# Layer 0 of a four-layer graph network: weighted sum by rows, the gate's sum on VectorE, a fourth buffer for the adjacency

## The chip, the cores and the metric

The kernel runs on one core of a Trainium2 chip, as one program. The metric is the device time of one execution in microseconds, the median of several runs. A core has a matrix engine (TensorE, PE in the profile, with its weight loads shown apart as PEld), a vector engine (VectorE, DVE), an activation engine (ScalarE, ACT), a general engine (GpSimd, POOL) and an engine that mostly issues transfers (SyncE, SP). Each runs its own instructions in order; they wait for one another by semaphores. SBUF is the on-chip memory, PSUM the memory into which PE writes its products. Transfers are issued here from SP and from POOL.

## The reference, cut to what matters

There are 16 graphs (batches) of 1024 nodes with 128 features each, and a 1024x1024 adjacency of zeros and ones per graph, symmetric and with a full diagonal. Four layers follow one another, each with a residual and a layer norm. The change touches the first one, which computes per batch:

```python
h = x @ W_w.T + W_b
e = jnp.einsum('bjl,bkl->bjk', h @ A, h)
e = e + jnp.swapaxes(e, 1, 2)
att = jnp.where(adj > 0, e, -9e15)
att = softmax(att, axis=1) * adj
h_prime = relu(einsum('bij,bjk->bik', att, h))
coeff = sigmoid(concatenate([x, h_prime], axis=-1) @ gate_w.T + gate_b)
x = layernorm(x + coeff * x + (1 - coeff) * h_prime)
```

The scores are symmetric before the softmax, so a row of them can be normalised where a column is meant. The gate is one number per node: 256 products, 128 with x and 128 with h', and a sum. Layer 1 first removes neighbours from the adjacency in an iterative way (the dilation), and then runs three aggregations with batch norms; layers 2 and 3 are another attention and a graph convolution. Nothing in them is changed except the number of buffers of one small pool in the dilation.

## The kernel before, in words

A batch has NT = 8 tiles of P = 128 nodes. Layer 0 is written as three Python generators per batch, which are run in turns ("rounds"): each `yield n` hands the turn to the other streams and comes back n rounds later. In round order the streams are `before(b + 1)`, `attention(b)` and `after(b - 1)`, so that the preparation of one batch, the attention of the next and the end of the one before go on at once. The order in which instructions are emitted, with a planner's reordering within each engine, fixes the order on each engine.

`before(b)` loads x (`xn`, L925, issued on SP) and eight pieces of the adjacency (`an`, 128x1024, L930, also on SP). ACT turns each piece into 8-bit numbers in the large buffer `Y` (printed as `carry`) and sums it to the degree (L931). DVE compares each piece with its mirror image, for a check of symmetry, in rows of several lengths: one against SBUF (L936) and one or two against PSUM (L944), into which PE has written transposed blocks (L943). On the way PE transposes x (L759), ACT copies it to `xT` (L950), PE and ACT make `G` (L766, L954), PE makes the x half of the gate in `gates` (L775, then L780), and PE and DVE make `hn`, the rows of h (L962, L963). At the end POOL stores the 8-bit adjacency (L965).

`attention(b)` takes the eight tiles one after another (`jt`): ACT makes a mask (L980), PE the scores of 128 rows against 1024 columns in two halves (L724), DVE adds the mask and takes the row minimum (`em`, L983), ACT the exponential with its row sum (L985), DVE the reciprocal `rs` (L987) and `hs`, 128 rows of h divided by that sum (L989). `weigh`, called one tile late, multiplies `hs` with `em` and adds up in `acc` in PSUM over the eight tiles (L973): `hs` is the stationary operand, two halves of 512 columns of `em` are streamed, and the result stands with features on the partitions and nodes along the row.

`after(b)` closes a batch. The relu (L1001, ACT) writes `hpT`, features on partitions. Three rounds later `gates` multiplies it with the h' half of the gate's vector in four column tiles of PE (L775), ACT copies the result out (L777), PE transposes it (L780) and DVE adds the x half, `gx` (L1005). ACT's tanh (L1007) and two small DVE rows (L1009, L1010) give the factors `cx` and `co` per node. Three rounds later DVE multiplies x by `cx` (L1013), PE transposes `hpT` back in eight blocks (L759), DVE multiplies these by `co` (L1015) and adds (L1016). Four rounds later, in round 10 of the 17 that `attention` takes, comes the layer norm (`normed`: statistics L794 and L796 on DVE, a power on POOL L745, L799 on DVE, eight rows L801 on ACT), and POOL stores the result (L1019). The next x load on SP reuses that buffer and so waits for that store.

PSUM holds two buffers of 1024 columns for the scores (`l0_pw`), one for `acc`, and two of 512 columns (`l0_ph`), which the transposes, G, h and the gates share. `an` has three buffers, `xn` three, `em` two. After layer 0 the score pools are closed and the dilation begins (`prepare` and what follows from L1063); the end of the last batch, `after(15)`, runs among its first instructions. There POOL computes a power over all degrees (L1188), which is in POOL's queue ahead of the last layer norm's power.

Of the kernel before, what the change touches and what calls it, by code (L numbers as in the profile page):

```python
# [9 lines left out]
F32 = mybir.dt.float32  # L10
# [5 lines left out]
FP8 = mybir.dt.float8e4  # L16
# [6 lines left out]
P = 128  # L23
# [616 lines left out]
def fast_kernel(ctx: ExitStack, tc: tile.TileContext, t: dict, out: bass.AP, flag: bass.AP):  # L640
# [46 lines left out]
    def nat(ap):  # L687
        return ap.rearrange("(t p) d -> p t d", p=P)
# [39 lines left out]
    def tiles3(ap):  # L728
        return ap.rearrange("p (t d) -> p t d", d=P)
# [24 lines left out]
    def turned(psum, src, tag="h"):  # L754

        for p, c, blocks in halves(psum, tag):
            for i, k in enumerate(blocks):
                s = src[:, k, :] if len(src.shape) == 3 else src[:, k * P:(k + 1) * P]
                nc.tensor.transpose(p[:, i * P:(i + 1) * P], s, identf)  # L759
            yield p, c, slice(blocks[0], blocks[-1] + 1)  # L760
# [8 lines left out]
    def gates(psum, out, *pairs):  # L769


        p = psum.tile([P, N // 4], F32, name="pq", tag="h")
        for i, (g, x) in enumerate(pairs):
            for q in range(4):
                nc.tensor.matmul(p[32 * q:32 * q + 32, :], g, x[:, q * N // 4:(q + 1) * N // 4], start=(i == 0),  # L775
                                 stop=(i == len(pairs) - 1), tile_position=(0, 32 * q))
        nc.scalar.copy(out, p)  # L777
        p = psum.tile([P, 2, P], F32, name="pg", tag="h")
        for t in range(2):
            nc.tensor.transpose(p[:, t, :], out[:, t * P:(t + 1) * P], identf)  # L780
        return p.rearrange("p t (q g) -> p q t g", q=4)

    def half_rows(v):

        return v[:, :, None].to_broadcast([P, 4, P])
# [124 lines left out]
    work = ending.enter_context(tc.tile_pool(name="l0_work", bufs=1, reuse_waits="tile"))  # L910
    small = ending.enter_context(tc.tile_pool(name="l0_small", bufs=2, reuse_waits="tile"))
    b0 = row_bcast(wts, t["L0_gnn_W_b"], P, "l0brow")
    gw = wts.tile([P, 2, 32], F32, name="l0gw")
    nc.vector.memset(gw, 0.0)
    with nc.allow_non_contiguous_dma(reason="a vector of 256"):
        nc.sync.dma_start(gw[:, :, 0], t["L0_gnn_gate_w"].rearrange("o (h d) -> d (o h)", d=P))
    gb = row_bcast(wts, t["L0_gnn_gate_b"], 1, "l0gb")
    gbh = wts.tile([P, 1], F32, name="l0gbh")
    nbig = wts.tile([P, 1], F32, name="l0nbig")
# [2 lines left out]
    def before(s, b):  # L922

        s.xn = work.tile([P, NT, P], F32, name="xn", bufs=3)
        nc.sync.dma_start(s.xn, nat(t["x"][b]))  # L925
        yield 1
        for it in range(NT):
            c = b * NT + it
            an = early.tile([P, N], F32, name="an", bufs=3)
            nc.sync.dma_start(an, t["adj"][b][it * P:(it + 1) * P, :])  # L930
            nc.scalar.activation(Y[b][:, it, :], an, AF.Copy, accum_out=deg[:, c:c + 1], saturate=False)  # L931

            chk = early.tile([P, N], FP8, name="chk")
            done = (it + 1) * P
            if done < N:
                nc.vector.scalar_tensor_tensor(chk[:, done:], an[:, done:], 0.0, an[:, done:], op0=OP.is_gt,  # L936
                                               op1=OP.not_equal, accum_out=other[:, b, it:it + 1], saturate=False)
            for h in range(it // 4 + 1):
                js = range(4 * h, min(4 * h + 4, it + 1))
                k = slice(js[0] * P, (js[-1] + 1) * P)  # L940
                pt = ps_h.tile([P, 512], F32, name="pt", tag="h")
                for i, jt in enumerate(js):
                    nc.tensor.matmul(pt[:, i * P:(i + 1) * P], Y[b][:, jt, it * P:done], identb, start=True, stop=True)  # L943
                nc.vector.scalar_tensor_tensor(chk[:, k], pt[:, :k.stop - k.start], 0.0, an[:, k], op0=OP.is_gt,  # L944
                                               op1=OP.not_equal, accum_out=other[:, b, 7 + it + 4 * h:8 + it + 4 * h],
                                               saturate=False)
            if it == (2 if b else 0):
                s.xT = work.tile([P, N], F32, name="xT", bufs=2)
                for p, c, _ in turned(ps_h, s.xn):
                    nc.scalar.copy(s.xT[:, c], p)  # L950
            if it == (4 if b else 1):
                s.G = work.tile([P, N], F32, name="G", bufs=2)
                for p, c in products(ps_h, (M0, s.xT)):
                    nc.scalar.activation(s.G[:, c], p, AF.Identity, scale=-1.0, bias=nu)  # L954
                pz = gates(ps_h, early.tile([P, N], FP8, name="chk").bitcast(F32), (gw[:, 0, :], s.xT))
                s.gx = small.tile([P, NT], F32, name="gx")
                nc.vector.tensor_copy(s.gx.rearrange("p (q t) -> p q t", t=2), pz[:, :, :, 0])
            if it == (5 if b else 2):
                s.hn = work.tile([P, N], F32, name="hn")
                for p, c, blocks in halves(ps_h):  # L960
                    for i, k in enumerate(blocks):
                        nc.tensor.matmul(p[:, i * P:(i + 1) * P], s.xT[:, k * P:(k + 1) * P], W0T, start=True, stop=True)  # L962
                    nc.vector.tensor_add(tiles3(s.hn[:, c]), tiles3(p), b0[:, None, :].to_broadcast([P, 4, P]))  # L963
            yield 2
        nc.gpsimd.dma_start(adj8_d[b], Y[b].bitcast(F32))  # L965

    def attention(s, b):
        s.acc = ps_a.tile([P, N], F32, name="acc")

        def weigh(jt, hs, em):  # L970
            for h in range(H2):
                c = slice(h * 512, (h + 1) * 512)
                nc.tensor.matmul(s.acc[:, c], hs, em[:, c], start=(jt == 0), stop=(jt == NT - 1))  # L973

        for jt in range(NT):
            js = slice(jt * P, (jt + 1) * P)
            c = b * NT + jt
            mn = mx0[:, c:c + 1]
            msk = work.tile([P, N], BF16, name="msk", bufs=2)
            nc.scalar.activation(msk, Y[b][:, jt, :], AF.Identity, scale=-BIG, bias=nbig)  # L980
            e = wide_matmul(ps_w, s.G[:, js], s.xT)
            em = work.tile([P, N], F32, name="em", bufs=2)
            nc.vector.tensor_tensor_reduce(em, e, msk, 1.0, 3.0e38, op0=OP.add, op1=OP.min, accum_out=mn)  # L983
            sm = small.tile([P, 1], F32, name="sm")
            nc.scalar.activation(em, em, AF.Exp, scale=-1.0, bias=mn, accum_out=sm)  # L985
            rs = small.tile([P, 1], F32, name="rs")
            nc.vector.reciprocal(rs, sm)  # L987
            hs = small.tile([P, P], F32, name="hs")
            nc.vector.tensor_scalar(hs, s.hn[:, js], rs, None, op0=OP.mult)  # L989
            yield  # L990
            if jt:
                weigh(*late)
            late = jt, hs, em
            yield
        weigh(*late)
        yield

    def after(s, b):

        hpT = work.tile([P, N], F32, name="hpT")  # L1000
        nc.scalar.activation(hpT, s.acc, AF.Relu)  # L1001
        yield 3
        pz = gates(ps_h, work.tile([P, NT, P], F32, name="r").rearrange("p t d -> p (t d)")[:, :N // 4], (gw[:, 1, :], hpT))
        co = small.tile([P, NT], F32, name="co")
        nc.vector.tensor_add(co.rearrange("p (q t) -> p q t", t=2), pz[:, :, :, 0],  # L1005
                             s.gx.rearrange("p (q t) -> p q t", t=2))
        nc.scalar.activation(co, co, AF.Tanh, scale=0.5, bias=gbh)  # L1007
        cx = small.tile([P, NT], F32, name="cx")
        nc.vector.tensor_scalar(cx, co, 0.5, 1.5, op0=OP.mult, op1=OP.add)  # L1009
        nc.vector.tensor_scalar(co, co, -0.5, 0.5, op0=OP.mult, op1=OP.add)  # L1010
        yield 3
        r = work.tile([P, NT, P], F32, name="r")
        nc.vector.tensor_mul(s.xn, s.xn, per_row(cx))  # L1013
        for p, c, k in turned(ps_h, hpT):
            nc.vector.tensor_mul(r[:, k, :], tiles3(p), half_rows(co[:, k]))  # L1015
        nc.vector.tensor_add(s.xn, s.xn, r)  # L1016
        yield 4
        normed(small, s.xn)
        nc.gpsimd.dma_start(nat(x1_d[b]), s.xn)  # L1019
        yield  # L1020
# [13 lines left out]

    with ExitStack() as ph:
        sb = ph.enter_context(tc.tile_pool(name="dl_sb", bufs=2, side="right", reuse_waits="tile"))
        tiny = ph.enter_context(tc.tile_pool(name="dl_small", bufs=3, side="right", reuse_waits="tile"))
        ps_b = ph.enter_context(tc.tile_pool(name="dl_pb", bufs=1, space=PSUM, side="right", reuse_waits="tile"))
        ps_d = ph.enter_context(tc.tile_pool(name="dl_pd", bufs=1, space=PSUM, side="right", reuse_waits="tile"))
        ps_s = ph.enter_context(tc.tile_pool(name="dl_ps", bufs=2, space=PSUM, side="right", reuse_waits="tile"))  # L1040
# [826 lines left out]
```

## Time and profile before

| what | value |
|---|---|
| median of 3 runs | 2696.75 us (2693.25 to 2697.32) |
| the profiled execution | 2694.93 us, span 2693.2 us, PE clock 0.983 of full speed |
| relu of batch 0, of batch 15 | 57.9 us, 624.9 us |
| a steady turn, relu to relu | 37.5 us |
| busy in one such turn (405.86 to 443.38) | PE all of it, ACT 33.3, DVE 30.2, POOL 3.2 us |
| issue to landing, median | `an` 3.7, x load 4.4, 8-bit adjacency store 4.2 us |

The profile is one execution. Line numbers (L973) are those of the kernel before. A row of the timeline has the start, the length, the engine, the line, the operation, what goes out and what comes in, the shapes and the count; in brackets the idle time of the engine before it and the engine that ended it. A row of the waits has who waited for whom, with the sum in us, the count and the longest. A row for a stretch of time has the busy time and the number of instructions of PE, PEld, DVE, ACT and POOL, then the clock that PE was granted, the share of the DMA engines and their GB/s. Lengths of single instructions contain time that overlaps the next one; the distance from one start to the next is what an engine spends on it.

### The profile page before, as it was taken

The page shows a single profiled execution, that of the slowest core. Times are in us where ns is not written, and L with a number is a line of the kernel's source. Part 1 is how long each engine was busy: PE and PEld are TensorE (multiplying, and loading weights), DVE is VectorE, ACT ScalarE, POOL GpSimd, SP SyncE. Part 2 cuts the span into 40 slices and gives each one's busy share as a digit, 9 for nine tenths or more (in the row PEclk, how much of TensorE's full clock was granted, in tenths as well). Part 3 has the DMA queues.
Part 4 walks back from the last instruction along what each step waited for, and adds up shares of the span by engine and source line. Part 5 has one row for each costly group of instructions (what it writes and reads, how often), then busy time and mean ns, then how long its engine had stood idle before and what let it go on. Part 6 is the DMA issues. An engine that isn't in the chain of part 4 may idle for free.

```text
span 2693.2 us, 41450 instructions
## 1 busy us (share of the span) xinstructions
PE 2539.0 (94%) x14888; PEld 1677.9 (62%) x14888; DVE 2085.4 (77%) x5590; ACT 1977.5 (73%) x3188; POOL 317.7 (12%) x287
## 2 busy tenths in 40 slices
PE   8999999997888869999999998999999999999986
PEld 4444454444666648887788885566566666666655
DVE  6887778876898877777688875678778777887885
ACT  7888889885988866666655534777777777777773
POOL 0000000003000001111122132001100100001010
PEclk9999999998999989999999998999999999999998
DMA  6555555530000052233366673102122111111100
GB/s 191 157 180 172 164 172 168 168 121 21 2 3 2 2 212 87 95 118 128 132 230 238 228 263 132 40 32 79 67 85 77 63 63 63 63 63 63 47 24 25
DMA packets 120807, 285.34 MB, mean 106 GB/s; under 512 B 12304, under 2 KB 65424, under 8 KB 113424
## 3 DMA queue, kind: packets, MB, share of 16 engines
q1 hardware_dynamic: 101280, 203.33, 23.1%
q0 software_dynamic: 19312, 79.28, 7.6%
q8 instruction: 119, 1.95, 0.3%
q14 instruction: 96, 0.79, 0.1%
HBM read 202.72 MB, written 79.82 MB: 105 GB/s over the span
## 4 chain that ended last, share of the span: by engine, by line
PE 58%; DVE 16%; issue 6%; ACT 4%; POOL 4%; DMA 2%; POOLq 0%; ACTq 0%; DVEq 0%
PE ph L1619 8%; PE acc L1679 7%; PE acc L1307 7%; PE ph L766 5%; PE acc L973 5%; PE pmm L724 5%; PE ph L759 4%; PE ph L1433 4%; PE pmm L1691 3%; PE ph L1606 2%; DVE mid L1097 2%; DVE keep L1148 2%; POOL ln_rstd L745 1%; POOL rn L745 1%; ACT q L1145 1%
## 5 line engine op out<-in xcount | busy, mean ns | idle before, releaser
L745 POOL TENSOR_TENSOR ln_rstd<-ln_rstd,mhalf 128x8 f32<-128x8 f32 (+1 forms) x68 | 108.3, 1593 | 1318.7 <-DVE ln_rstd L742 864.2
L973 PE MATMUL acc<-em,hs 128*128 128x512 f32 x512 | 259.3, 607 | 2.5 <-DVE past L1075 1.3
L724 PE MATMUL pmm<-xT,G 128*128 128x512 f32 x512 | 259.8, 604 | 0.0
L1679 PE MATMUL acc<-ex,hs 128*128 128x512 f32 x512 | 248.9, 596 | 7.5 <-DVE hs L1706 4.6
L801 ACT ACTIVATE xn<-xn,ln_nb,ln_rstd 128x128 f32<-128x128 f32 x512 | 204.6, 481 | 61.1 <-DVE ln_nb L799 61.0
L1307 PE MATMUL acc<-a,hi 128*128 128x512 f32 x768 | 232.7, 396 | 11.5 <-DVE a L1294 8.5
L1307 PE MATMUL acc<-a,lo 128*128 128x512 f32 x768 | 230.3, 394 | 5.9 <-DVE lo L1274 5.8
L985 ACT ACTIVATE em<-em,mx 128x1024 f32<-128x1024 f32 x128 | 146.3, 1143 | 54.0 <-DVE mx L983 52.7
L983 DVE CUSTOM_DVE_ANT_0 em<-pmm,msk 128x1024 f32<-128x1024 f32 x128 | 156.1, 1219 | 31.9 <-PE pmm L724 30.8
L1699 ACT ACTIVATE ex<-em,mn 128x1024 f32<-128x1024 f32 x128 | 146.9, 1148 | 44.7 <-DVE mn L1696 44.0
L1691 PE MATMUL pmm<-G,hT 128*128 128x512 f32 (+3 forms) x416 | 175.3, 523 | 0.1
L1696 DVE CUSTOM_DVE_ANT_0 em<-pmm,msk 128x1024 f32<-128x1024 f32 x128 | 155.4, 1214 | 24.4 <-PE pmm L1693 22.3
L1307 PEld LDWEIGHTS acc<-a,lo 128*128 128x128 f32 x768 | 143.1, 189 | 41.2 <-DVE lo L1274 12.0
L1307 PEld LDWEIGHTS acc<-a,hi 128*128 128x128 f32 x768 | 141.8, 189 | 42.9 <-DVE a L1294 11.0
L1157 ACT ACTIVATE carry<-pc,negone 128x1024 fp8e4<-128x1024 f32 x128 | 141.4, 1116 | 26.2 <-PE pc L1156 23.2
L931 ACT ACTIVATE carry<-an 128x1024 fp8e4<-128x1024 f32 x128 | 134.5, 1051 | 30.5 <-DMA an<-in_adj 29.7
L980 ACT ACTIVATE msk<-carry,l0nbig 128x1024 bf16<-128x1024 fp8e4 x128 | 145.4, 1136 | 0.0
L1619 PE MATMUL ph<-A,hi 128*128 128x512 f32 x512 | 143.1, 420 | 1.2 <-DVE zn L1608 0.7
L1687 ACT ACTIVATE msk<-A,nbig 128x1024 bf16<-128x1024 fp8e4 x128 | 144.2, 1137 | 0.0
L1296 ACT CAST a<-A 128x1024 fp32r<-128x1024 fp8e4 x96 | 98.4, 1048 | 54.3 <-PE acc L1307 52.7
L1679 PEld LDWEIGHTS acc<-ex,hs 128*128 128x128 f32 x512 | 88.6, 190 | 76.8 <-issue 54.6
L1296 ACT CAST a<-carry 128x1024 fp32r<-128x1024 fp8e4 x96 | 99.1, 1047 | 47.1 <-PE acc L1307 46.8
(319 smaller groups left out, 6185.2 us busy)
## 6 DMA issues: line engine op xcount, KB each, us to landing
an<-in_adj SPq DMA_DIRECT2D x128, 512.0 KB, 3.7
adj_d<-carry POOLq DMA_DIRECT2D x16, 1024.0 KB, 4.2
A<-dil_d SPq DMA_DIRECT2D x16, 1024.0 KB, 5.3
rdeg<-rdeg_d SPq DMA_DIRECT2D x32, 512.0 KB, 3.9
A<-adj_d SPq DMA_DIRECT2D x16, 1024.0 KB, 4.8
ag_d<-ag POOLq DMA_DIRECT2D x24, 512.0 KB, 5.0
ag<-ag_d SPq DMA_DIRECT2D x24, 512.0 KB, 5.3
xn<-in_x SPq DMA_DIRECT2D x16, 512.0 KB, 4.4
```

The lines of the kernel that those rows point to most:

```text
L724: nc.tensor.matmul(p[:, h * 512:(h + 1) * 512], lhsT, rhs[:, h * 512:(h + 1) * 512], start=True, stop=True)
L745: nc.gpsimd.tensor_tensor(r, r, mhalf[:, :n], op=OP.pow)
L801: nc.scalar.activation(r[:, k.start + i, :], r[:, k.start + i, :], AF.Identity, scale=rstd[:, i:i + 1], bias=nb[:, i:i + 1])
L973: nc.tensor.matmul(s.acc[:, c], hs, em[:, c], start=(jt == 0), stop=(jt == NT - 1))
L983: nc.vector.tensor_tensor_reduce(em, e, msk, 1.0, 3.0e38, op0=OP.add, op1=OP.min, accum_out=mn)
L1296: nc.scalar.copy(a, A[:, 2 * i:2 * i + 2, c])
L1307: nc.tensor.matmul(acc, part[:, jt, :], pieces[h * NT // 2 + k][:, jt - 2 * k, :], start=(part is parts[0] and jt == 0), stop=(part is par ...
L1619: nc.tensor.matmul(p, part[:, jt, :], A[jt][:, c], start=(jt == 0 and i == 0), stop=(jt == NT - 1 and i == 1))
L1679: nc.tensor.matmul(s.acc[:, c], hs, ex[:, c], start=(jt == 0), stop=(jt == NT - 1))
L1691: nc.tensor.matmul(e[:, c], s.hT[:, js], s.G[:, c], start=True, stop=True)
L1696: nc.vector.tensor_tensor_reduce(row, e, msk, 1.0, 0.0, op0=OP.add, op1=OP.min, accum_out=mn)
L1699: nc.scalar.activation(ex, row, AF.Exp, scale=-1.0, bias=mn, accum_out=sm)
```

## The change

`weigh` now takes a 128x128 block of `em` as the stationary operand and streams `hs`, so that there are eight products of 128 columns per tile instead of two of 512, and `acc` has nodes on the partitions and features along the row. The relu so writes `hp` by rows. The h' half of the gate is computed on DVE, for each of the eight blocks a multiplication with the gate's vector in all partitions (`ghrow`, a new small load) and a sum along the row (L1006 of the new kernel), two rounds behind the relu instead of three. There is no second `gates`, no copy of it and no transposes back; `hp` is multiplied by `co` in one instruction of 128x1024 (new L1014), in place, and added (new L1015). The layer norm comes in round 15 instead of 10. `an` has four buffers, the x load is issued on POOL for batches above 2, the gate's weights `gw` hold the x half only, and the dilation's small pool has two buffers instead of three.

```diff
-    gw = wts.tile([P, 2, 32], F32, name="l0gw")
+    gw = wts.tile([P, 32], F32, name="l0gw")
     nc.vector.memset(gw, 0.0)
-    with nc.allow_non_contiguous_dma(reason="a vector of 256"):
-        nc.sync.dma_start(gw[:, :, 0], t["L0_gnn_gate_w"].rearrange("o (h d) -> d (o h)", d=P))
+    nc.sync.dma_start(gw[:, 0:1], t["L0_gnn_gate_w"][:, :P].rearrange("o d -> d o"))
+    ghrow = row_bcast(wts, t["L0_gnn_gate_w"][:, P:], P, "l0gh")
...
-        nc.sync.dma_start(s.xn, nat(t["x"][b]))
+        (nc.gpsimd if b > 2 else nc.sync).dma_start(s.xn, nat(t["x"][b]))
...
-            an = early.tile([P, N], F32, name="an", bufs=3)
+            an = early.tile([P, N], F32, name="an", bufs=4)
...
-            for h in range(H2):
-                c = slice(h * 512, (h + 1) * 512)
-                nc.tensor.matmul(s.acc[:, c], hs, em[:, c], start=(jt == 0), stop=(jt == NT - 1))
+            for k in range(NT):
+                c = slice(k * P, (k + 1) * P)
+                nc.tensor.matmul(s.acc[:, c], em[:, c], hs, start=(jt == 0 and k % 4 == 0), stop=(jt == NT - 1 and k % 4 == 3))
...
-        hpT = work.tile([P, N], F32, name="hpT")
-        nc.scalar.activation(hpT, s.acc, AF.Relu)
-        yield 3
-        pz = gates(ps_h, work.tile([P, NT, P], F32, name="r").rearrange("p t d -> p (t d)")[:, :N // 4], (gw[:, 1, :], hpT))
+        hp = work.tile([P, NT, P], F32, name="hp")
+        nc.scalar.activation(hp, tiles3(s.acc), AF.Relu)
+        yield 2
+        r = work.tile([P, P], F32, name="r")
         co = small.tile([P, NT], F32, name="co")
-        nc.vector.tensor_add(co.rearrange("p (q t) -> p q t", t=2), pz[:, :, :, 0],
-                             s.gx.rearrange("p (q t) -> p q t", t=2))
+        for i in range(NT):
+            nc.vector.scalar_tensor_tensor(r, hp[:, i, :], 1.0, ghrow, op0=OP.mult, op1=OP.mult, accum_out=co[:, i:i + 1])
+        nc.vector.tensor_add(co, co, s.gx)
         nc.scalar.activation(co, co, AF.Tanh, scale=0.5, bias=gbh)
...
-        yield 3
-        r = work.tile([P, NT, P], F32, name="r")
+        yield 4
         nc.vector.tensor_mul(s.xn, s.xn, per_row(cx))
-        for p, c, k in turned(ps_h, hpT):
-            nc.vector.tensor_mul(r[:, k, :], tiles3(p), half_rows(co[:, k]))
-        nc.vector.tensor_add(s.xn, s.xn, r)
-        yield 4
+        nc.vector.tensor_mul(hp, hp, per_row(co))
+        nc.vector.tensor_add(s.xn, s.xn, hp)
+        yield 9
         normed(small, s.xn)
...
-        tiny = ph.enter_context(tc.tile_pool(name="dl_small", bufs=3, side="right", reuse_waits="tile"))
+        tiny = ph.enter_context(tc.tile_pool(name="dl_small", bufs=2, side="right", reuse_waits="tile"))
```

More of the change, by code (lines that the diff above doesn't have):

```diff
@@ L954, in before @@
                     nc.scalar.activation(s.G[:, c], p, AF.Identity, scale=-1.0, bias=nu)
-                pz = gates(ps_h, early.tile([P, N], FP8, name="chk").bitcast(F32), (gw[:, 0, :], s.xT))
+                pz = gates(ps_h, early.tile([P, N], FP8, name="chk").bitcast(F32), (gw, s.xT))
                 s.gx = small.tile([P, NT], F32, name="gx")
```

## The prediction

> **What bounds the kernel now.** I read the page's totals and its chain first, to see which engine sets the end.
>
> ```profile
> PE 2539.0 (94%) x14888; PEld 1677.9 (62%) x14888; DVE 2085.4 (77%) x5590; ACT 1977.5 (73%) x3188; POOL 317.7 (12%) x287
> ...
> PE 58%; DVE 16%; issue 6%; ACT 4%; POOL 4%; DMA 2%; POOLq 0%; ACTq 0%; DVEq 0%
> ...
> L973 PE MATMUL acc<-em,hs 128*128 128x512 f32 x512 | 259.3, 607 | 2.5 <-DVE past L1075 1.3
> ```
>
> TensorE carries the chain, and the line to be changed, L973, never waits inside layer 0. But these are averages, so I went to the stage. Layer 0 repeats one turn per batch; I measure it from one relu (L1001) to the next. These start at 57.9, 104.1, 142.2, 180.5, then every 37.5 us to 593.6, and last at 624.9. Next, one steady turn's busy times (PE, PEld, DVE, ACT, POOL), then its waits, then single instructions on PE, DVE, POOL and SP.
>
> ```profile
> 405.86:443.38 37.52, 37.52 (x158) 18.51 (x157) 30.23 (x98) 33.26 (x58) 3.17 (x3) 1.00 0.53 169
> ```
>
> ```profile
> DVE rs L987 <- ACT em L985: 4.9, 3, 2.0
> ...
> ACT carry L931 <- DMA an<-in_adj: 1.1, 2, 0.6
> ```
>
> ```profile
> 410.73 0.64 PE L775 MATMUL pq<-hpT,l0gw 128*32 128x256 f32 x8
> 411.30 1.12 PE L724 MATMUL pmm<-xT,G 128*128 128x512 f32 x2
> ...
> 416.16 0.60 PE L759 MATMUL ph<-identf,hpT 128*128 128x128 f32 x4
> 416.60 1.02 PE L724 MATMUL pmm<-xT,G 128*128 128x512 f32 x2
> ...
> 432.02 1.95 PE L962 MATMUL ph<-l0WT,xT 128*128 128x128 f32 x16
> 433.80 1.02 PE L973 MATMUL acc<-em,hs 128*128 128x512 f32 x2
> ```
>
> ```profile
> 409.81 0.29 DVE L944 SCALAR_TENSOR_TENSOR chk<-pt,an 128x128 fp8e4<-128x128 f32 x1
> 410.02 0.09 DVE L944 DVE_READ_ACCUMULATOR chk<-pt,an 128x1 bf16 x1
> 410.02 0.16 DVE L987 RECIPROCAL rs<-sm 128x1 f32<-128x1 f32 x1
> ```
>
> ```profile
> 433.20 0.91 POOL L1019 DMA_DIRECT2D x_d<-xn  x1 [3.88 <-ACT xn L801]
> ```
>
> ```profile
> 438.00 0.38 SPq L925 DMA_DIRECT2D xn<-in_x  x1
> ```
>
> ```profile
> 624.10 20.74 POOL L1188 TENSOR_TENSOR deg<-deg,mhalf 128x128 f32<-128x128 f32 x1 [5.87 <-DVE deg L1187]
> ...
> 646.49 0.17 DVE L799 SCALAR_TENSOR_TENSOR ln_nb<-ln_mv,ln_rstd 128x8 f32<-128x8 f32 x1 [5.80 <-POOL ln_rstd L745]
> ```
>
> The reader should see: PE is busy for the whole turn at full clock, DVE is free for 7 of its 37.5 us and ACT for 4, and an adjacency piece is late by at most 0.6 us without PE waiting. So PE instructions set the turn, until another engine is late. The starts in the PE rows give pitches: 416.16 to 416.60 is 0.11 us per transpose; 416.60 to 417.46 (the next row) is 0.43 per 512-column record; 432.02 to 433.80 is 0.111 for each of 16 records of L962. A block multiply of 128 columns on DVE shows 0.29 us but its successor starts 0.21 later.
>
> **What the Trainium skill says.** "FP8 and Floating Point Precision", TensorE Precision Notes: true FP32 takes four passes through the array. The trace agrees: a 512-column product is two records of 0.43, 0.86 us, which is four times 512 columns at 2.4 GHz (0.853). "TensorE: Matmul & The Clock Gate", Step-by-step: the next weights load while the current matmul runs. L962 agrees: a new 128x128 block of weights for each product and still 0.22 us per product. "VectorE: DVE Perf Modes", The TRN2 errata: (N+151)/0.96 ns for a two-operand fp32 operation, 291 ns at 128. The row's 0.29 agrees; start to start it is less, and I use the trace. "DMA: Bandwidth & Descriptors", Latency and other measured facts: first byte about 1 us from GpSimd against 0.6 us from Sync; the issues above (0.91 and 0.38) lean the same way.
>
> **The change, part by part**, per steady turn, durations from that turn.
> Removed on PE: the h' half of the gate, 8 records of L775, 0.57 with 0.2 for going into and out of column tiles, together 0.78; two L780 transposes, 0.22; eight L759 transposes of hpT, 0.87. Sum 1.87.
> Added on PE: L973 gives 64 products of 128 columns for 16 of 512. L962 has the same shape with changing weights, so 64 × 0.2225 = 14.24 against 32 × 0.429 = 13.73: +0.51. No trace shows this shape alternating with 512-column products. From below, equal streaming costs 0; from above, 0.24 per product gives +1.6. I take +0.51. Net on PE: -1.36, a turn of 36.16 if PE keeps streaming.
> ACT loses the copy of L777, 0.35. It has 4 us to spare; nothing gained.
> DVE loses two L1015 multiplies (0.64 each) and gains one of 1024 (1.15, as L1013) and eight block sums. One has the form of the check's 128-column row, 0.21 to 0.22 each. Bounds: no less than 0.15 (128 columns and the shortest neighbours), no more than 0.41 (0.29, an accumulator read of 0.085 and a hand-over, if nothing overlaps). I take 0.22: +1.76. DVE goes from 30.4 to 32.1 of 36.2.
>
> That fits as a sum, not everywhere: `yield 2` puts the sums early. In the new order all eight lie before the fifth minimum (L983) of the turn. Behind the first, which can start when the relu ends (relu + 1.04), come up to that minimum's end: 8 sums 1.76, 4 hs 0.88, 3 rs 0.37, check rows from PSUM 3 × 0.60 + 0.21 + 0.35 + 0.47 = 2.83, check rows from SBUF 1.02 + 0.88 + 0.74 + 0.60 + 0.47 = 3.71, 4 minima 4.66, the gate's small rows 0.35, the multiplies by cx and co 2.30. Sum 16.9, so it ends at relu + 17.9. It frees a score buffer that PE wants after 9 half-scores (7.72), 32 products of L973 (7.12), about 26 check transposes (1.45), 8 transposes of x (0.87) and switches (0.5): relu + 17.7. PE is 0.25 late. The check row behind it holds a PSUM slot for G (L953) and costs another 0.2. So the turn is 36.16 + 0.45 = 36.6, a saving of 0.9, and each 0.01 on a block sum costs 0.08.
>
> Transfers: the fourth adjacency buffer takes away at most the waits above, which PE doesn't feel, so 0 in a steady turn. The x load moves to POOL behind the x1 store. The norm now comes in round 15, in the new ACT order its eight rows stand one exponential later than before, where they ended at 432.9, relu + 27; with some 4 us per exponential they end near relu + 31, the store issues there and lands 4.2 later; then 0.91 to issue and some 4 to land gives relu + 40, about 3 into the next turn. The first transpose of it is at 7.5. It is hidden with 4 us to spare; it delays on POOL only the layer-norm power and the carry store, both over 10 us away. SP no longer stands at 438.00 for the store, so pieces can be issued earlier.
> The two `tiny` buffers of the dilation: no wait appears or goes on any compute engine in the order, so 0; if its 67 rounds each waited 0.1, +7.
>
> The sum over layer 0: turns 1 to 3 (46.2, 38.2, 38.2) gain like the others, -3 together: the first waits on transfers, and what it gives away the fourth buffer should return (0 to -6). Ten steady turns × 0.9 = -9. The fourteenth holds the late norm: -0.3. The last (31.3) has PE's -1.4 (+1 to -2.5). At the boundary DVE stands 5.8 us for POOL's power chain, which covers the extra sums of the last `after`; its degree power follows the last hs and moves 0.6 earlier relative to the relu: -0.6. Total -14.3. Against the profiled 2694.9 that is 2680.6; the median of the runs lies 1.8 higher, so 2682.5. Behind layer 0 each engine has the same order as before.
>
> **Rivals.**
> 1. PE's full gain: DVE's 0.45 is not lost, because a sum costs 0.17 rather than 0.22 or PE has overheads I haven't placed. 14 × 1.36 and the ends: 2676. For it: the lateness is small. Against: two slots bind at once.
> 2. The gain is eaten. Either a product in L973 takes 0.24 (64 × 0.0175 = 1.1 per turn, no more than 0.2 left) or a sum takes 0.31 (8 × 0.09 = 0.7). With the first turns' -3, 2692 to 2697. For it: neither form stands in the trace in this mix. Against: L962 and the check rows.
> 3. Slower: DVE paces the turn. If every block sum takes 0.41, lateness grows by 8 × 0.19 = 1.5 beyond the 0.45, the turn is 38.1, +0.6, with the ends +9: 2706. It decides from 0.33 per sum, where the turn is 37.5 again. For it: each sum also writes an accumulator, and all write one buffer r. Against: in the new order mostly another instruction stands between two of them, and the check's accumulator read costs 0.02 start to start.
> 4. The x load on POOL comes late: it needs 4 us more than counted; then PE waits in every turn. The share is inside rival 3's.
>
> **Chances.** The forecast, 2682.5 with its own range 2676 to 2690: 63%. Full gain 14%. Eaten 13%. Slower 10%. A measurement of this kernel tells about 0.2%, 5.4 us, from no change: faster is below 2691.4, slower above 2702.1. The first two cases are faster; of the third most lies within, a part faster. Range: below, rival 1 with more from the first turns, 2671; above, all of rival 2, 2700, which leaves out the slower case and little else.
>
> **What will show it.** Relu to relu of 36.4 to 36.9 in the steady turns; L973's records 0.111 apart; L1006 0.22 start to start; PE waiting 0.2 to 0.5 per turn on DVE at L724 and L766 and nowhere on DMA; the x load landing some 4 us before its transposes; the second and third turns below 37. The forecast is wrong if L973's pitch is 0.115 or more, if L1006 needs over 0.3, or if a gain in layer 0 is given back behind the degree power.

## The result and the profile after

The changed kernel takes 2682.28 us (median of six runs, 2680.62 to 2685.05), the kernel before, run beside it, 2696.94 us (2693.25 to 2697.32). The ratio is 0.995, with an interval of 0.994 to 0.996: 14.7 us faster. The forecast was 2682.5. The profiled execution took 2682.24 us with a span of 2680.4 us, 12.8 us less in span than the one before; that one lay 2 us under the median of its kernel, so the two profiles show a little less than the medians do.

The table sets the forecast's sum against the two traces. The first row goes up to the start of turn 4, the fourth relu; in brackets stand the first relu and then turns 1 to 3.

| term | forecast | measured |
|---|---|---|
| first relu and turns 1 to 3 | -3 | -2.4 (+1.7, +1.3, -3.7, -1.7) |
| ten steady turns | -9 | -7.9 (36.76 instead of 37.55 each) |
| the fourteenth turn | -0.3 | +0.6 |
| the last turn | -1.4 | -2.7 |
| boundary to the dilation | -0.6 | -0.6 |
| behind layer 0 | 0 | +0.3 (-13.05 at its start, -12.8 at the end) |
| sum | -14.3 | -12.7 (of the spans themselves: -12.8) |

First the page's totals and the chain that ended last, then the two groups of L973 from the costliest ones, here the weight loads and the products.

```profile
PE 2521.3 (94%) x16136; PEld 1800.2 (67%) x16136; DVE 2102.6 (78%) x5830; ACT 1969.3 (73%) x3172; POOL 330.8 (12%) x300
...
PE 52%; DVE 19%; ACT 11%; issue 8%; POOL 4%; DMA 3%; POOLq 0%; ACTq 0%; DVEq 0%; SPq 0%
...
L973 PEld LDWEIGHTS acc<-hs,em 128*128 128x128 f32 x2048 | 248.7, 192 | 37.9 <-issue 26.8
L973 PE MATMUL acc<-hs,em 128*128 128x128 f32 x2048 | 269.1, 279 | 0.7 <-DVE hs L989 0.3
```

PE is busy for 17.7 us less with 1248 records more, DVE for 17.2 us more. PE still carries the chain, with a share of 52% instead of 58%: the others have come nearer. The weight loads of L973 now take 248.7 us, but the products show no wait for them: they idle for 0.7 us in all of layer 0.

Busy times (PE, PEld, DVE, ACT, POOL), clock and transfers of two steady turns, a longer one and a clean one:

```profile
361.30:398.60 37.30, 36.86 (x237) 26.19 (x235) 31.39 (x114) 32.70 (x56) 4.52 (x5) 1.00 0.51 170
398.60:435.10 36.50, 36.44 (x238) 26.18 (x235) 31.30 (x114) 32.82 (x58) 4.17 (x5) 1.00 0.52 174
```

The clean turn is 36.5 us where it was 37.5; DVE has gone from 30.2 to 31.3, ACT from 33.3 to 32.8. Single instructions of the clean turn on PE, then on DVE:

```profile
410.48 0.33 PE L943 MATMUL pt<-identb,carry 128*128 128x128 bf16 x3
410.65 2.01 PE L973 MATMUL acc<-hs,em 128*128 128x128 f32 x16
412.49 0.28 PE L943 MATMUL pt<-identb,carry 128*128 128x128 bf16 x2
412.60 1.94 PE L724 MATMUL pmm<-xT,G 128*128 128x512 f32 x4
414.37 1.95 PE L973 MATMUL acc<-hs,em 128*128 128x128 f32 x16
416.38 1.98 PE L724 MATMUL pmm<-xT,G 128*128 128x512 f32 x4
```

```profile
405.63 0.29 DVE L1006 SCALAR_TENSOR_TENSOR r<-hp,l0gh 128x128 f32<-128x128 f32 x1
405.84 0.08 DVE L1006 DVE_READ_ACCUMULATOR r<-hp,l0gh 128x1 f32 x1
405.84 1.22 DVE L983 CUSTOM_DVE_ANT_0 em<-pmm,msk 128x1024 f32<-128x1024 f32 x1
...
415.10 1.22 DVE L983 CUSTOM_DVE_ANT_0 em<-pmm,msk 128x1024 f32<-128x1024 f32 x1
416.24 0.08 DVE L983 DVE_READ_ACCUMULATOR2_ANT mx<- 128x1 f32 x1
```

From 410.65 to 412.49 are 16 records of L973, 1.84 us, of which 0.06 is the step from bf16 to f32: 0.111 each. From 414.37 to 416.38 it is 2.01, 0.23 more than 16 such records: here PE stands until the minimum that started at 415.10 has ended, at 416.24 to 416.32. It is the one that the forecast counts as the fifth, the fourth to start behind the relu. That is the one wait that the forecast placed. A block sum starts at 405.63 and its successor at 405.84, 0.21 later; the accumulator's read shows a length but costs no start.

### The profile page after: what moved, and what is told of

It is laid out like the page before. It is cut to its first block, busy times and chain, and to the rows that moved or that the text cites. A ratio compares the mean times of both kernels' runs of the same rounds, so it can differ in the third digit from the quotient of the medians.

```text
span 2680.4 us, 44092 instructions
## 1 busy us (share of the span) xinstructions
PE 2521.3 (94%) x16136; PEld 1800.2 (67%) x16136; DVE 2102.6 (78%) x5830; ACT 1969.3 (73%) x3172; POOL 330.8 (12%) x300
## 4 chain that ended last, share of the span: by engine, by line
PE 52%; DVE 19%; ACT 11%; issue 8%; POOL 4%; DMA 3%; POOLq 0%; ACTq 0%; DVEq 0%; SPq 0%
PE ph L1618 8%; PE acc L1678 7%; PE acc L1306 7%; PE ph L766 6%; PE ph L1432 4%; PE ph L759 3%; PE pmm L1690 3%; PE acc L973 2%; PE pmm L724 2%; ACT em L985 2%; PE ph L1605 2%; ACT xn L801 2%; DVE mid L1096 2%; DVE keep L1147 2%; POOL ln_rstd L745 2%
## 5 line engine op out<-in xcount | busy, mean ns | idle before, releaser
L973 PEld LDWEIGHTS acc<-hs,em 128*128 128x128 f32 x2048 | 248.7, 192 | 37.9 <-issue 26.8
L973 PE MATMUL acc<-hs,em 128*128 128x128 f32 x2048 | 269.1, 279 | 0.7 <-DVE hs L989 0.3
L724 PE MATMUL pmm<-xT,G 128*128 128x512 f32 x512 | 251.4, 604 | 1.4 <-DVE mx L983 0.7
L983 DVE CUSTOM_DVE_ANT_0 em<-pmm,msk 128x1024 f32<-128x1024 f32 x128 | 155.9, 1218 | 35.1 <-PE pmm L724 32.8
```

Of the source, the lines that this page charges most:

```text
L724: nc.tensor.matmul(p[:, h * 512:(h + 1) * 512], lhsT, rhs[:, h * 512:(h + 1) * 512], start=True, stop=True)
L973: nc.tensor.matmul(s.acc[:, c], em[:, c], hs, start=(jt == 0 and k % 4 == 0), stop=(jt == NT - 1 and k % 4 == 3))
```

## The experiments

Each kernel is the changed one with the edit shown, unless the kernel before is named. Every ratio is to the kernel before on the same chip.

### Is it the order of the work? The pauses of before, and the norm alone

e1 takes the three pauses of `after` from the kernel before, so that the gate and the norm come in its rounds, and keeps all else. The planner orders the engines anew.

```diff
-        yield 2
+        yield 3
...
-        yield 4
+        yield 3
...
-        yield 9
+        yield 4
```

> The changed kernel with the pauses of the kernel before: gate three rounds behind the relu, then 3, norm after 4 (round 10 instead of 15). Every instruction stays, only the order on the engines moves. Theory A, the time comes from the instructions taken off PE: the steady turn stays 36.4 to 37.3 us and the whole at 2682, within 5. Theory B, the pauses are what lets PE keep streaming: in the new order the norm's statistics and its eight ACT rows fall where G and hn of the next batch are made, the bank for hn's products comes free late, and PE stands more than 1 us per turn; turn about 37.9, the last turn 3 us longer, the whole 2698 to 2703, no better than before.

Measured: 2691.48 us, ratio 0.9984 (0.9975 to 0.9993). The steady turn is 37.44 us on average, the last 31.9: of 14.7 us some 10 are gone, though PE, DVE and ACT have the same instructions to do. In turns 4 to 13 DVE now stands for 12.0 us at L799 for POOL's power, and PE for 7.6 us at L962 for DVE's check rows, right behind that stop.

e7 moves the layer norm alone, with the other two pauses as changed.

```diff
-        yield 9
+        yield 4
```

> The changed kernel with the norm four rounds behind the multiplies, in round 10, instead of nine; the gate stays two rounds behind the relu. Theory A, where the norm stands does not matter: total 2682 to 2684. Theory B, in round 10 the norm's rows on DVE and ACT stand in front of the work that frees the banks for hn and the check: PE late by more than 1 us, turns 37.8 to 38.4, the last turn 3 longer, total 2696 to 2704.

Measured: 2696.93 us, ratio 1.0003 (0.9994 to 1.0012). The norm's place alone takes back the whole gain; the steady turn is 37.71. Here are the waits of ten turns (from 178.0 to 545.6 us; sum, count, longest), and DVE and PE in one turn:

```profile
DVE ln_nb L799 <- POOL ln_rstd L745: 14.8, 10, 1.8
...
PE pt L943 <- DVE gx L957: 4.2, 5, 1.1
PE acc L973 <- DVE hs L989: 3.6, 6, 0.6
```

```profile
354.45 0.17 DVE L742 TENSOR_SCALAR ln_rstd<-ln_mv 128x8 f32<-128x8 f32 x1
356.48 0.17 DVE L799 SCALAR_TENSOR_TENSOR ln_nb<-ln_mv,ln_rstd 128x8 f32<-128x8 f32 x1 [1.85 <-POOL ln_rstd L745]
356.56 1.22 DVE L983 CUSTOM_DVE_ANT_0 em<-pmm,msk 128x1024 f32<-128x1024 f32 x1
357.70 0.16 DVE L957 COPY gx<-pg 128x8 f32<-128x8 f32 x1
```

```profile
357.92 0.27 PE L943 MATMUL pt<-identb,carry 128*128 128x128 bf16 x2 [0.79 <-DVE gx L957]
```

Some 25 us after the relu DVE stands 1.85 us for POOL, with a row minimum and the copy of `gx` queued behind; the copy frees the PSUM buffer that PE wants for its transposes, and PE is 0.79 us late. Every other turn is like this. In the turns between, the stop is 1.1 us and PE is 0.41 us late at L962 behind it; but there PE also stands 0.77 us at 16 to 18 us after the relu, for `hs` and a minimum, ahead of the stop. So the stop explains some 0.6 of the 1.0 us that PE stands per turn; the rest comes with the order that the planner makes around the moved norm, and was not followed.

The kernel before had the norm in the same round, but stood there for 3.7 us in ten turns, the changed one not at all. In e1 the norm is in round 10 too, and some 5 us of the gain are left: the pauses work together. A stop on DVE costs by what is queued behind it: e3, below, which has 1.7 us less to do on DVE per turn, stands there for 18.2 us in ten turns at no loss against the changed kernel.

### Is it the work taken off PE?

e8 is the kernel before without the h' half of the gate: about 1.0 us less on PE per turn (the term is left out of the result), with no sum on DVE in its place.

```diff
-        pz = gates(ps_h, work.tile([P, NT, P], F32, name="r").rearrange("p t d -> p (t d)")[:, :N // 4], (gw[:, 1, :], hpT))
...
-        nc.vector.tensor_add(co.rearrange("p (q t) -> p q t", t=2), pz[:, :, :, 0],
-                             s.gx.rearrange("p (q t) -> p q t", t=2))
+        nc.vector.tensor_copy(co, s.gx)
```

> Leaves out part of the computation: in the kernel before, the h' half of the gate (eight L775, the copy on ACT, two transposes on PE, the addition); the factors come from x alone. PE has 1.0 us less per turn, ACT 0.35, DVE 0.08. Theory A, PE sets the turn, whatever the order: 36.5 us, total down by 13 to 15. Theory B, what the planner makes of it decides, and a wait takes the place of the work: turn 37.5 to 37.9, total 2694 to 2700.

Measured: 2695.97 us, ratio 1.0002 (0.9993 to 1.0011), steady turn 37.74. Less work on PE, and nothing won: DVE stands 18.4 us in ten turns for POOL's power, and PE 4.1 us for `hs`. That is 0.4 of the 1.2 us per turn to be explained (1.0 us less work, a turn 0.2 us longer); where the rest goes was not followed. Leaving instructions out also lets the planner arrange the rest anew, so this isn't the old order with a hole in it.

e4 weighs by columns again in the changed kernel and reads the result as if it stood by rows: 0.5 us less on PE per turn.

```diff
-            for k in range(NT):
-                c = slice(k * P, (k + 1) * P)
-                nc.tensor.matmul(s.acc[:, c], em[:, c], hs, start=(jt == 0 and k % 4 == 0), stop=(jt == NT - 1 and k % 4 == 3))
+            for h in range(H2):
+                c = slice(h * 512, (h + 1) * 512)
+                nc.tensor.matmul(s.acc[:, c], hs, em[:, c], start=(jt == 0), stop=(jt == NT - 1))
```

> Leaves the meaning of the computation: the weighted sum is multiplied by columns again (two products of 512 per tile), and what follows reads it as if it stood by rows; all else as in the changed kernel, no transposes back. PE has 0.5 us less per turn (13.73 for 14.24). Theory A, PE sets the turn alone: 36.1, total down by 7. Theory B, DVE sets it together with PE, so that PE's saving turns into a longer wait for the minimum: turn 36.5 to 37.4, total not below that of the changed kernel.

Measured: 2699.93 us, ratio 1.0012 (1.0005 to 1.0019), turns of 37.4 to 39.9. Its waits, same stretch:

```profile
ACT carry L931 <- DMA an<-in_adj: 28.4, 23, 2.4
...
PE ph L759 <- ACT xT L950: 7.4, 8, 1.3
PE acc L973 <- DVE hs L989: 5.5, 7, 1.1
```

Cheaper products, and some 17 us slower than the changed kernel: adjacency pieces are late for 28.4 us (5.2 in the changed kernel), and PE waits behind what ACT does after them. Neither kernel keeps the order of its parent, so order and work aren't separated here. But in both PE's saving is lost, and the waits shown are for DVE, ACT and transfers: it counts only where these keep pace.

e3 leaves the block sums out (the h' term of the gate is missing).

```diff
-        for i in range(NT):
-            nc.vector.scalar_tensor_tensor(r, hp[:, i, :], 1.0, ghrow, op0=OP.mult, op1=OP.mult, accum_out=co[:, i:i + 1])
-        nc.vector.tensor_add(co, co, s.gx)
+        nc.vector.tensor_copy(co, s.gx)
```

> Leaves out part of the computation: the h' half of the gate (the eight block sums on DVE), the factors come from x alone. DVE has 1.7 us less per turn, all of it ahead of the turn's fifth minimum. Theory A, those sums make DVE late by 0.2 to 0.5 us per turn and nothing else does: turn 36.2, the gap at L724 and L766 gone, total 2677. Theory B, the gap belongs to PE: turn 36.6 as before. Theory C, the planner orders the rest anew and a new stall appears elsewhere: turn 36.9, total about the same as the changed kernel.

Measured: 2681.95 us, ratio 0.9946 (0.9929 to 0.9962), later turns 36.67 (36.90 over turns 4 to 13). The 1.7 us of sums per turn on DVE cost nothing net. It doesn't prove them free in the order of the changed kernel, since the planner gives another one without them: here PE has waits of 2.5 us on `hs` in ten turns, and DVE stands 18.2 us at L799.

### Is it the transfers? The fourth buffer and the place of the x load

```diff
-            an = early.tile([P, N], F32, name="an", bufs=4)
+            an = early.tile([P, N], F32, name="an", bufs=3)
```

> The changed kernel with three buffers for the adjacency's pieces; the planner moves a few rows with it. Theory A, the fourth buffer works in the first turns only: steady turns as in the changed kernel (36.4 to 37.3 us), total up by 0 to 3. Theory B, in the new order ACT takes up to three pieces one right behind the other, so that pieces come late in steady turns too: 36.9 us and more, total up by 4 to 10.

Measured for e5: 2686.87 us, ratio 0.9968 (0.9957 to 0.998). The steady turn is 37.25 and the last relu of layer 0 starts at 617.3 instead of 612.5: 4.9 us, spread over the steady turns at 0.5 each. In its waits:

```profile
ACT carry L931 <- DMA an<-in_adj: 4.7, 9, 1.5
...
PE pt L943 <- ACT carry L931: 3.8, 7, 1.4
```

ACT waits no longer than with four buffers (4.7 against 5.2 us), but now PE waits behind it, at the transposes. The planner orders e5 anew on all engines, so the buffer and the order that comes with it aren't separated. e6 gives the fourth buffer to the kernel before (the small norm statistics have one buffer in layer 0, to make room).

```diff
-            an = early.tile([P, N], F32, name="an", bufs=3)
+            an = early.tile([P, N], F32, name="an", bufs=4)
```

> The kernel before with four buffers for the adjacency's pieces and nothing else of the change (to make room, the statistics of layer 0's norm have one buffer instead of two). Theory A, the buffer alone takes away the waits for pieces, 0.6 us at most each, which PE does not feel: turn 37.4 to 37.5, the first two turns 1 to 2 us shorter, total 2693 to 2697. Theory B, a good part of the change's 14 us comes from it: 2690 or less.

Measured: 2696.53 us, ratio 1.0004 (0.9995 to 1.0012), steady turn 37.53. Nothing: ACT waits for pieces as long with four buffers (9.4 us in ten turns) as with three (9.0), and eight of its ten turns take 37.4 us. So the fourth buffer is worth something only in the changed kernel; whether because of its shorter turn or because of its order wasn't tried.

```diff
-        (nc.gpsimd if b > 2 else nc.sync).dma_start(s.xn, nat(t["x"][b]))
+        nc.sync.dma_start(s.xn, nat(t["x"][b]))
```

> The changed kernel with every x load issued on SP again; the order on PE, DVE and ACT is the same. Theory A, the queue of the x load does not matter since it lies 4 us ahead of its use: turns and total as in the changed kernel, within 2 us. Theory B, the longer turns of the changed kernel (37.3 us, PE 0.5 to 0.8 us late at the second half of the x transposes behind an adjacency piece) come from where the x load stands: on SP it stands ahead of the pieces and waits for the store, the pieces behind it come later, and turns are 0.5 to 2 us longer, total up by 5 to 20.

Measured for e2: 2683.85 us, ratio 0.9954 (0.9937 to 0.997), steady turn 36.80. No difference from the changed kernel that the runs can tell; the order on the compute engines is the same.

e12 has three `an` buffers like e5, and four for x, so that each x load comes a turn ahead of its use (`r` in bf16 makes the room).

```diff
-        s.xn = work.tile([P, NT, P], F32, name="xn", bufs=3)
+        s.xn = work.tile([P, NT, P], F32, name="xn", bufs=4)
...
-            an = early.tile([P, N], F32, name="an", bufs=4)
+            an = early.tile([P, N], F32, name="an", bufs=3)
...
-        r = work.tile([P, P], F32, name="r")
+        r = work.tile([P, P], BF16, name="r")
```

> The changed kernel with three buffers for the adjacency's pieces and four for x (the scratch row of the block sums in 16 bit, to make room), so that the x load no longer waits for the store and lands a turn earlier; the order on PE, DVE and ACT is that of the run with three buffers. Theory A, turns are long where the x load lands beside the pieces that ACT takes next: here the pieces come in time, no turn over 37.0, total 2680 to 2684, 3 to 6 less than with three buffers. Theory B, pieces are late because three buffers are few for that order, wherever the x load is: turns and total as with three buffers, 2687.

Measured: 2688.12 us, ratio 0.9975 (0.9968 to 0.9983), steady turn 37.21, as e5. The x load issued at 402.4 is now used at 449.3, where in e5 the one issued at 400.9 is used at 410.6, and nothing is won: the x load's spare time isn't what makes these turns longer. But each load is still issued behind a store, with the wait of e5 (32.4 us there):

```profile
POOL xn L925 <- DMA x_d<-xn: 32.9, 10, 3.7
```

So the load runs in the same part of the turn as in e5, and e12 doesn't test whether its traffic makes the pieces beside it late.

### The dilation's small pool

```diff
-        tiny = ph.enter_context(tc.tile_pool(name="dl_small", bufs=2, side="right", reuse_waits="tile"))
+        tiny = ph.enter_context(tc.tile_pool(name="dl_small", bufs=3, side="right", reuse_waits="tile"))
```

> The changed kernel with three buffers in the dilation's small pool; the order on PE, DVE and ACT is the same. Theory A, the third buffer was never waited for: total as in the changed kernel, within 2 us. Theory B, two buffers cost waits in the 67 rounds of the dilation: total down by 3 to 7, all of it between the last relu of layer 0 and the first of layer 2.

Measured: 2684.55 us, ratio 0.9956 (0.994 to 0.9973). No effect that the runs can tell.

### Further on the same way: the x half of the gate without column tiles

e9 computes the x half of the gate as a 129th column of the products for `hn` and needs no `gates` at all: some 1.5 us less on PE per turn. Its pauses are 3, 3, 9.

```diff
+        W0g = wts.tile([P, P + 1], F32, name="l0Wg")
+        nc.vector.tensor_copy(W0g[:, :P], transposed(raw, ps_h, W0, "l0WT", "h"))
...
+    nc.sync.dma_start(W0g[:, P:], t["L0_gnn_gate_w"][:, :P].rearrange("o d -> d o"))
...
+                        nc.tensor.matmul(v[:, i, :], s.xT[:, k * P:(k + 1) * P], W0g, start=True, stop=True)
+                    nc.vector.tensor_add(tiles3(s.hn[:, k0 * P:(k0 + n) * P]), v[:, :, :P], b0[:, None, :].to_broadcast([P, n, P]))
+                    nc.vector.tensor_copy(s.gx[:, k0:k0 + n], v[:, :, P])
```

> A further step on the changed kernel: the x half of the gate comes out of the products that make hn, with the gate's vector as a 129th column (three banks of 3, 3 and 2 blocks instead of two of 4), so that the last column-tiled products, their copy on ACT and two transposes go; gate three rounds behind the relu, then 3, norm after 9. PE has some 1.5 us less per turn (0.57 of products, 0.7 of gaps at the column tiles, 0.22 of transposes), ACT 0.25. Theory A, with an order in which no long wait stands, PE's saving is seen in part: turn 36.0 to 36.3, total 2673 to 2678. Theory B, DVE or ACT now pace the turn: 36.6 or more, total 2682 or more.

Measured: 2684.74 us, ratio 0.9957 (0.994 to 0.9973), no faster than the changed kernel. Its shortest turns are 35.96 us, but others reach 39.9, and the mean is 36.99. Its waits in the same stretch:

```profile
ACT carry L931 <- DMA an<-in_adj: 34.0, 27, 2.5
...
PE acc L973 <- DVE hs L989: 8.0, 14, 2.1
...
PE ph L759 <- DMA xn<-in_x: 1.9, 4, 0.7
```

PE's saving is there in the shortest turns. But the pieces are late for 34.0 us instead of 5.2, and the x load too reaches PE. The wait for `hs`, PE's longest in sum, can come from a piece: in the turn of 39.0 us ACT starts a piece 2.37 us late at 392.11, its exponential follows, DVE's reciprocal waits 1.85 us for that, and PE 1.70 us for the `hs` behind it. So transfers share in setting the turn. DVE also stands 18.5 us for POOL at L799 here; what that adds wasn't tried, nor whether a fifth buffer would help.

e10 is e9 with the changed kernel's pauses, 2, 4, 9.

> The same instructions as in the run with the gate's x half made with hn, but with the pauses of the changed kernel (2, 4, 9). Theory A, the pauses are a property of the kernel and 2, 4, 9 is good here too: turn 36.0 to 36.3, total 2673 to 2678. Theory B, which pauses are good depends on the instructions around them: in this order PE waits for DVE 1.6 us per turn, turn 37.2, total 2683 to 2690.

Measured: 2691.23 us, ratio 0.9983 (0.9976 to 0.9989), steady turn 38.11. In ten turns PE stands 12.1 us for `hs` instead of 8.0; DVE's stop for POOL is the same 18.5 us, and pieces are late for 24.9. The pauses that suit one set of instructions cost 6.5 us with another.

No kernel tried is clearly faster than the changed one.

## Why the prediction was right, point by point

**PE's sum held.** In the turn from 398.6 the starts on PE give L973 15.01 us with the wait of 0.23 in it, against 14.29 in a turn before: +0.49, forecast +0.51. The parts taken out were those priced. Without its lateness the clean turn is 36.1, forecast 36.16. The record's pitch is 0.111, so rival 2's product of 0.24 isn't there.

**DVE's lateness held.** The fifth minimum ends 17.7 us after the relu (forecast 17.9), and PE stands 0.20 to 0.23 in every steady turn before L724 (forecast 0.25). The PSUM slot of G cost 0.12 (four records of L766 take 1.84 instead of 1.72; forecast 0.2). As this lateness is in every steady turn, rival 1 is out. A block sum takes 0.213 in the median, so rival 3, from 0.33 on, and the second half of rival 2 are out. DVE's total in the forecast, from 30.4 to 32.1 us, starts above the 30.23 of the row that it shows; measured is 31.3.

**The x load held.** It is issued 0.8 us before the relu and lands about 4 after it; its first transpose is at relu + 7.4. On POOL:

```profile
393.66 0.94 POOL L1018 DMA_DIRECT2D x_d<-xn  x1 [6.14 <-ACT xn L801]
397.82 0.89 POOL L925 DMA_DIRECT2D xn<-in_x  x1 [3.22 <-DMA x_d<-xn]
```

The spare is 3.4 us, forecast 4. Rival 4 is out, and by e2 the queue doesn't matter.

**The step that was wrong: "The fourth adjacency buffer takes away at most the waits above, which PE doesn't feel, so 0 in a steady turn"**, and with it "nowhere on DMA". With three buffers the steady turn is 0.5 us longer (e5). Even with four, lateness gets through to PE in most turns. In the turn from 361.3, on ACT and then on PE:

```profile
367.06 1.06 ACT L931 ACTIVATE carry<-an 128x1024 fp8e4<-128x1024 f32 x1 [0.48 <-DMA an<-in_adj]
...
370.19 0.56 ACT L950 COPY xT<-ph 128x512 f32<-128x512 f32 x1
```

```profile
370.81 0.65 PE L759 MATMUL ph<-identf,xn 128*128 128x128 f32 x4 [0.36 <-ACT xT L950]
```

The piece is 0.48 us late; ACT's copy of `xT` comes behind it in its queue and frees the PSUM buffer for the second four transposes of x. Start to start, PE loses 0.52 us there. Six of the ten steady turns have a late piece at this place, some 5 us after the relu, and each shows the same gap: 0.18, 0.18, 0.26, 0.37, 0.48 and 0.78 us late give gaps of 0.22, 0.23, 0.31, 0.41, 0.52 and 0.65. The other four, at 36.43 to 36.48, have none there; in three of them a piece is late by 0.72 to 0.98 some 25 us after the relu, and PE doesn't feel it. The gaps are 0.23 us per turn on average. Two errors thus partly cancel: the turns without a gap are 0.15 shorter than the forecast's 36.6, and the ten together, at 36.76, are 0.16 longer.

The pieces aren't later than before: ACT waits for them 5.2 us in the ten turns, and 9.0 in the kernel before. There one is 0.33 to 0.65 us late in every steady turn some 6.5 us after the relu, as here on ACT:

```profile
412.46 1.06 ACT L931 ACTIVATE carry<-an 128x1024 fp8e4<-128x1024 f32 x1 [0.65 <-DMA an<-in_adj]
...
414.84 0.56 ACT L950 COPY xT<-ph 128x512 f32<-128x512 f32 x1
```

PE's second four transposes of x start at 414.87, while that copy still runs, so they don't wait for it. In the new order they do. The view of waits named ACT as the one that waits for the DMA; who waits for ACT had to be followed further. What failed is "which PE doesn't feel": it was true of the old order and was carried over to the new one, which the forecast had followed for DVE, but not for what stands behind a late piece on ACT.

**The ends.** The first relu and the first turn lost 3.0 us where a gain was expected, and the second turn returned it at once (34.4 us); why the first relu comes 1.7 us later wasn't tried, and the fourth buffer doesn't settle it: e6, with that buffer alone, has it at 60.0 instead of 57.9, but e5, with three, at 59.0. The fourteenth and last turns together gave -2.05, forecast -1.7; the split differs. The fourteenth has the same gap before L759, 0.78 us, and was priced without it. The last turn goes with the norm's place: it takes 31.2 to 31.9 us in each kernel with the norm in round 10 (before, e1, e6, e7, e8), whatever PE has to do, and 28.6 to 30.2 in each with round 15. The forecast had put its -1.4 down to PE's work. The boundary's -0.6 held.

**What the right number hides.** That 2682.5 was met within 0.2 us is luck: in span the gain is 12.8 us and not 14.3, and the profiled execution of the kernel before lay 2 us under its median, the one after at it. The forecast put the gain down to PE's work less a little lateness, and got near the sum. By e7 the same work is worth nothing with the norm in round 10, and by e8 less work was worth nothing in the kernel before. The sum came near because the new order was followed row by row to see what DVE has to do before the fifth minimum, and that order had no stop on POOL in it. The forecast used the norm's new round only to time the x load and the fourteenth turn; that it is worth as much as the whole gain was not foreseen. Had the order had e7's stop, "PE carries the chain" would have given the same forecast and missed by 14 us. That the late norm alone, in the kernel before, brings nothing is only argued: PE never waited there.

## What to carry to other kernels

Where the next engines are nearly as busy as the bounding one, as DVE (30.2 us) and ACT (33.3 us) were here in a turn of 37.5, a saving on the bounding one is a ticket, not a gain: it is cashed only if the next engines and transfers keep pace with the shorter turn, so redo their lateness in the new order and for the new length, and not from waits of the old one. Follow an instruction that waits on a slow helper (here POOL's 1.7 us power) to what is queued behind it; moving the norm, which holds that wait, five rounds on was worth as much as the whole gain. And follow a late transfer through the engine that waits for it to the buffer which that engine was to free next.

## What was not expected of the hardware

Products of 128 f32 columns, each with new weights, keep 0.111 us per record (two records each) also when they alternate with 512-column ones and bf16 transposes; the weight loads' 248.7 us in L973 stay behind the products. A product of 128 f32 columns so takes 0.223 us, four times the 0.056 between two bf16 transposes of 128 columns, as the four passes named in the forecast have it. A 128-column DVE row with a sum is 0.28 to 0.29 us long, which agrees with an estimate of 291 ns from the formula (N+151)/0.96 in the Trainium skill's "VectorE: DVE Perf Modes", The TRN2 errata (the page has it measured at 512 and 2048 columns), but the next row starts after 0.213, and the accumulator's read of 0.085 is hidden in it, whatever the row's own length suggests. Going into column tiles for the gate's x half and out again leaves gaps of 0.09, 0.21, 0.30 and 0.10 us between starts on PE, 0.71 of the 0.77 us that the eight records cost.
